# Zero rows up to 128 in the operands of the bias and mask matmuls of an attention and state-space block

## The chip, the cores and the metric

The kernel runs on one NeuronCore of a Trainium2 chip. The metric is the device time of one execution in microseconds (us), as the median of several runs; lower is better. A core has five engines that work through queues of their own, in the order in which the program lists the instructions: TensorE (PE in the profile, with its weight loads as PEld), VectorE (DVE), ScalarE (ACT), GpSimd (POOL) and SyncE (SP), which here only starts transfers. They wait for each other through semaphores.

## The reference, cut to what matters

The input `x` has 128 batches of 64 positions with 256 channels, in f32. Two blocks follow each other. The first is linear attention with a key mask, the second a selective state-space block ("Mamba"). What bears on the change is in the first block, and in the gate of the second:

```python
xn = _layernorm(x, norm_scale, norm_bias)
q, k, v = xn @ Wq + bq, xn @ Wk + bk, xn @ Wv + bv
k = where(mask, -inf, k); v = where(mask, 0.0, v)      # mask[b, t]
q = softmax(q, over the 16 channels of a head); k = softmax(k, over positions)
y = einsum(q, einsum(k, v))                            # per head and batch
h = _layernorm(y, ...) * (1 + scale) + shift           # scale, shift from cond
x = x + silu(h) @ film_out_W + film_out_b
...
shift, scale, gate = split(silu(cond) @ W_ada + b_ada, 3)
x = x + gate * mamba(permuted(_layernorm(x) * (1 + scale) + shift))
```

The state-space block has 512 channels with 16 states each. Its recurrence runs over the 64 positions of a batch.

## The kernel before, in words

The 128 batches are worked through in 16 groups of eight (512 positions, four tiles of 128). For each group `prepare` computes the attention block and the inputs of the recurrence, two calls of `scan` run the recurrence for four batches each, and two calls of `finish` project back, gate and write out. The first group is prepared in two halves of two tiles each, so its tiles are half as wide.

All of this is recorded first and issued later. `Plan.record` notes each operation as a node with what it needs; several matmuls in one `with pl.unit()` make one node. The table `ORDER` gives each node of each part a due time by hand, `Plan.order` sorts by these (a node whose buffer is not free yet steps back), and `Plan.emit` issues the nodes in that order. So the profile shows one line, L485, for nearly everything, and the groups are told apart by the names of the tiles. The engines interleave the `prepare` of one group with the `scan` and `finish` of the group before.

Names that come up below:

- `kp` (in `prepare`): the transposed keys of the group in a PSUM bank of 512 columns, one for each half of the 256 channels. A first matmul writes the mask into the bank: `lhsT=ones[0:1, :]`, `rhs=mrow`, where `mrow` is one row of 512 bf16 values, 0 or -1e30. The matmuls of `wk` and `xT`, f32 with 128 rows, then add to it. `km`, `nb`, `kT`, `ks` are the steps of the softmax that follow, on DVE, POOL and ACT.
- `project` (from line 811): `qp` (queries), `op` (the output of the attention block) and `vp` (values). For `qp` and `op` the first matmul writes the bias: `lhsT=ones` (three rows), `rhs=third[bias]`, three bf16 rows whose sum is the f32 bias, used for two tiles at a time. `vp` has no bias there.
- `gp` (in `setup`): the gate of all batches, one such bias matmul.
- `turn` makes the transposes `xtp`, `qtp`, `htp`; `ktp` transposes the keys; `ap` is keys times values, `bd` its masked copy on DVE; `yps` is queries times that.
- `hb` (in `scan`): 64-row, 64-column matmuls, 512 columns wide, that bring the inputs of the recurrence into one of two PSUM buffers; DVE's TENSOR_TENSOR_SCAN (`hs` or `hb`) runs the recurrence on them with the `decay` that ACT computes; `hs<-hs,ct` and `hs<-hs` are products and sums on POOL; `yacc` gathers the outputs on PE, started by two bf16 matmuls with the zero tile `blank`.
- `dtp`, `dt`: the step sizes; ACT writes `dt`, DMAs take it to `dt_d` in DRAM and back as `dt` in another layout, and ACT's `decay` reads that.
- `xz`, `xp`, `zp`, `pd`, `bp`, `bT`, `utp`, `w`, `diag`: other steps of the state-space block. `dm`, `ve`, `mu`, `rt`: the layer norms' small steps on POOL, from the statistics `st` of DVE.

The banks `kp`, `qp`, `op`, `vp`, `ap`, `xp` and so on share three PSUM buffers in turn (`bank`).

Every matmul is described by its rows and columns in the array: 128 rows for the f32 projections, 64 for `hb`, three for the biases, one for the mask. The constants are made at the start of `block_kernel`: `ident`, `blank`, `bmask` and others by POOL, `ones` by DVE at line 538.

Of the kernel before, what the change touches and what calls it, by code (L numbers as in the profile page):

```python
# [10 lines left out]
BF16 = mybir.dt.bfloat16  # L11
# [6 lines left out]
B, T, D, E = 128, 64, 256, 512  # L18
H, DH = 16, 16
DI, DS, DTR, DC = 512, 16, 64, 4  # L20
P = 128
NB = 8
TG = NB * T
# [465 lines left out]
def block_kernel(  # L489
# [20 lines left out]
    nc = tc.nc  # L510
# [5 lines left out]
    def ctile(shape, name, dt=F32):  # L516
        return const.tile(shape, dt, name=name, tag=name)
# [5 lines left out]
    pl = Plan(tc)  # L523
# [6 lines left out]
    def kept(shape, name, dt=F32):  # L530
        return pl.held(ctile(shape, name, dt))
# [2 lines left out]
    make_identity(nc, ident)  # L534
    blank = ctile([P, 512], "blank", BF16)
    nc.gpsimd.memset(blank, 0.0)
    ones = ctile([3, P], "ones", BF16)
    nc.vector.memset(ones, 1.0)

    bmask = ctile([P, P], "bmask")  # L540
    nc.gpsimd.memset(bmask, 1.0)
# [2 lines left out]
        out=bm3, in_=bm3, pattern=[[-DH, P // DH], [0, DH]], base=0,  # L544
# [3 lines left out]
        out=bm3, in_=bm3, pattern=[[DH, P // DH], [0, DH]], base=DH - 1,  # L548
# [20 lines left out]
    def v(name, k):  # L569
        return vec[:, VOFF[name][0] + k : VOFF[name][0] + k + 1]  # L570
# [8 lines left out]
    nA = kept([P, NC * SJ], "nA")  # L579
    gsel = kept([P, P], "gsel")  # L580
    keep = kept([P, B * T // P], "keep")
    third = {n: kept([3, D], "third_" + n, BF16) for n in ("bq", "film_out_b", "b_gate")}
    mneg_d = pl.held(dram1.tile([B, T], BF16, name="mneg_d"))
    gate_d = pl.held(dram1.tile([B, D], F32, name="gate_d"))
    mod_d = pl.held(dram1.tile([P, 4, KD, B], F32, name="mod_d"))
# [4 lines left out]
    def tile_of(shape, name, tag, bufs, dt=F32):  # L590
        return pl.tile(wp, shape, name, tag, bufs, dt)

    def bank(name):
        return pl.tile(ps, [P, 512], name, "bank", NBANK)
# [10 lines left out]
    def small(name, shape):  # L605
        return tile_of(shape, name, name, 2)
# [12 lines left out]
    def by_batch(ap):  # L619
        return ap.rearrange("p (b t) -> p b t", t=T)  # L620
# [190 lines left out]
    def project(to, srcT, w, bias, i2):  # L811

        pp = to.rearrange("p (i c) -> p i c", c=D)
        with pl.unit():
            if bias is not None:
                pl.tensor.matmul(
                    pp, lhsT=ones, rhs=third[bias][:, None, :].to_broadcast([3, 2, D]),
                    start=True, stop=False,
                )
            for h in range(2):  # L820
                i = 2 * i2 + h
                for k in range(KD):
                    pl.tensor.matmul(
                        pp[:, h, :], lhsT=srcT[:, k, i * P : (i + 1) * P], rhs=w[:, k, :],
                        start=(bias is None and k == 0),
                        stop=(k == KD - 1 and (bias is None or h == 1)),
                    )
        return pp


    def prepare(g, lo=0, NT=NT):

        NB, TG = NT * (P // T), NT * P
        tiles, cols = slice(lo, lo + NT), slice(lo * P, (lo + NT) * P)
        first = (g * TILES + lo) * (P // T)
        if lo == 0:
# [8 lines left out]
        x_d, xz, dts, uts, bT, c_d = state[g]  # L845
        xt = g4("xt", [P, NT, D])
        pl.sync.dma_start(out=xt, in_=xin[g][:, tiles, :])
        mrow = tile_of([1, TG], "mrow", "mrow", 1, BF16)
        pl.sync.dma_start(
            out=mrow, in_=mneg_d[first : first + NB, :].rearrange("(o b) t -> o (b t)", o=1)  # L850
        )
        mods = small("mods", [P, 4, KD, NB])
        pl.sync.dma_start(out=mods, in_=mod_d[:, :, :, first : first + NB])
# [11 lines left out]
        for m in range(KD):  # L865
            kp = bank("kp")[:, :TG]
            with pl.unit():
                pl.tensor.matmul(kp, lhsT=ones[0:1, :], rhs=mrow, start=True, stop=False)
                for k in range(KD):
                    pl.tensor.matmul(  # L870
                        kp, lhsT=wk[:, k, m * P : (m + 1) * P], rhs=xT[:, k, :],
                        start=False, stop=(k == KD - 1),
                    )
            km = small("km", [P, NB])
            pl.vector.tensor_reduce(km, by_batch(kp), axis=AX.X, op=ALU.max)

            nb = small("nb", [P, NB])
            pl.gpsimd.tensor_scalar(nb, km, 1.0, v("bk", m), op0=ALU.mult, op1=ALU.add)
            pl.gpsimd.tensor_scalar(nb, nb, -1.0, v("bk", m), op0=ALU.mult, op1=ALU.add)
            kk = by_batch(kT[:, m, :])  # L880
            with pl.unit():
                for b in range(NB):
                    ts = slice(b * T, (b + 1) * T)
                    pl.scalar.activation(
                        kT[:, m, ts], kp[:, ts], AF.Exp, bias=nb[:, b : b + 1]
                    )
            ks = small("ks", [P, NB])
            pl.vector.tensor_reduce(ks, kk, axis=AX.X, op=ALU.add)
            pl.vector.reciprocal(ks, ks)
            pl.gpsimd.tensor_tensor(  # L890
                kk, kk, ks[:, :, None].to_broadcast([P, NB, T]), op=ALU.mult
            )
# [3 lines left out]
        for i2 in range(NT // 2):  # L896
            pp = project(bank("vp"), xT, wv, None, i2)
            for h in range(2):
                i = 2 * i2 + h
                pl.scalar.activation(  # L900
                    vt[:, i, :], pp[:, h, :], AF.Identity,
                    scale=keep[:, g * TILES + lo + i : g * TILES + lo + i + 1],
                )
# [4 lines left out]
        for i2 in range(NT // 2):  # L908
            pp = project(bank("qp"), xT, wq, "bq", i2)
            qm = small("qm", [P, 2 * H])  # L910
            p3 = pp.rearrange("p i (h e) -> p (i h) e", e=DH)
            pl.vector.tensor_reduce(qm, p3, axis=AX.X, op=ALU.max)
            q3 = qt[:, 2 * i2 : 2 * i2 + 2, :].rearrange("p i (h e) -> p (i h) e", e=DH)
            pl.vector.tensor_tensor(
                q3, p3, qm[:, :, None].to_broadcast([P, 2 * H, DH]), op=ALU.subtract
            )
            pl.scalar.activation(q3, q3, AF.Exp)
            pl.vector.tensor_reduce(
                qs[:, i2 * 2 * H : (i2 + 1) * 2 * H], q3, axis=AX.X, op=ALU.add
            )  # L920
# [21 lines left out]
        for k in range(KD):  # L942
# [3 lines left out]
            with pl.unit():  # L946
                for i in range(NT):
                    for h in range(2):
# [3 lines left out]
                            start=True, stop=True,  # L952
# [9 lines left out]
        for i2 in range(NT // 2):  # L962
            pp = bank("yps").rearrange("p (i c) -> p i c", c=D)
            with pl.unit():
                for hi in range(2):
                    i = 2 * i2 + hi
                    for h in range(2):
                        ts = slice(h * T, (h + 1) * T)
                        for k in range(KD):
                            pl.tensor.matmul(  # L970
                                pp[ts, hi, k * P : (k + 1) * P],
                                lhsT=qT[:, k, i * P + h * T : i * P + (h + 1) * T],
                                rhs=bd[k][:, h, i, :], start=True, stop=True,
# [15 lines left out]
        for i2 in range(NT // 2):  # L989
            xs = xt[:, 2 * i2 : 2 * i2 + 2, :]  # L990
            pp = project(bank("op"), hT, wfo, "film_out_b", i2)
            pl.vector.tensor_tensor(xs, xs, pp, op=ALU.add)
# [13 lines left out]
        for m in range(KI):  # L1006
            xp = bank("xp")[:, :TG]
            with pl.unit():
                for k in range(KD):
                    pl.tensor.matmul(  # L1010
                        xp, lhsT=win[:, k, m * P : (m + 1) * P], rhs=h1[:, k, :],
                        start=(k == 0), stop=(k == KD - 1),
# [14 lines left out]
        for m in range(KI):  # L1027
            zp = bank("zp")[:, :TG]
            with pl.unit():
                for k in range(KD):  # L1030
                    pl.tensor.matmul(
                        zp, lhsT=win[:, k, DI + m * P : DI + (m + 1) * P], rhs=h1[:, k, :],
                        start=(k == 0), stop=(k == KD - 1),
# [5 lines left out]
        with pl.unit():  # L1039
            for k in range(KI):  # L1040
                pl.tensor.matmul(
                    pd[: DTR + 2 * DS, :], lhsT=wxp[:, k, :], rhs=xc[k],
                    start=(k == 0), stop=(k == KI - 1),
# [14 lines left out]
        for m in range(KI):  # L1058
            vp = bank("dtp")[:, :TG]
            pl.tensor.matmul(  # L1060
                vp, lhsT=wdt[:, m * P : (m + 1) * P], rhs=xd[:DTR, :], start=True, stop=True,
# [153 lines left out]
    for g in range(NG):  # L1215
        if g == 0:
            for lo in range(0, NT, 2):
                pl.part(prepare, f"first{lo}", g, lo, 2)
        else:
            pl.part(prepare, "second" if g == 1 else "prepare", g)  # L1220
        when = {NG - 1: "_last", 0: "_first"}.get(g, "")
        for half in range(2):
            pl.part(scan, f"scan{half}{when}", g, half)
            pl.part(finish, f"finish{half}{when}", g, half)
# [55 lines left out]
```

## Time and profile before

| what | value |
|---|---|
| median of three runs | 1940.35 us |
| lowest and highest | 1938.8 and 1941.37 us |
| the profiled execution | 1942.74 us |
| its span in the profile | 1941.0 us |
| instructions in the trace | 32381 |
| mean granted clock of TensorE | 0.987 |
| matmuls `kp<-mrow,ones` | 34, of one row |
| matmuls `qp<-third_bq,ones` and `op<-third_film_out_b,ones` | 32 each, of three rows |
| matmul `gp<-third_b_gate,ones` | 1, of three rows |

The profile comes from one execution, recorded by the hardware. Times in it are us from the start of its span. A timeline lists, for one engine, the start of an entry, its length, the engine, the line, the operation, the tiles it writes and reads, the shapes (partitions x elements; for a matmul rows*columns of the array and then the moving operand) and how many equal instructions were merged into it. A bracket at the end gives the idle time before it and who ended it. The end of a matmul is modelled, and matmuls overlap: what one costs in a stream is read from start to start, not from its length.

### The profile page before, as it was taken

To read this page: it belongs to the slowest core of one execution; us is meant where nothing else is said; L and a number is where in the kernel's file an instruction comes from. 1 tells how busy PE (TensorE), PEld (TensorE's weight loads), DVE (VectorE), ACT (ScalarE), POOL (GpSimd) and SP (SyncE) were. 2 spreads that over 40 slices of the span, in tenths; PEclk is the share of its full clock that TensorE was granted. 3 is DMA by queue.
4 is the path that set the end of the run, shared out by engine and by line. 5 is a ranking of instruction groups with operands and counts; after the bars stand their busy time and mean duration, and the time that the engine had idled before them with its cause. 6 is when DMAs were issued, how large, how long until landed. Compare 5 with 4: busy or idle time off the path is not lost. (4 is left out here: it accounts for less than half of the span.)

```text
span 1941.0 us, 32381 instructions
## 1 busy us (share of the span) xinstructions
PE 1819.4 (94%) x11304; PEld 931.0 (48%) x11304; DVE 1775.8 (91%) x1626; ACT 1696.5 (87%) x3981; POOL 1778.1 (92%) x1468
## 2 busy tenths in 40 slices
PE   7799999999999999999999999999999999999777
PEld 5453554545455454544536454454545545454233
DVE  4589799999999999999999999899999999999796
ACT  4889799898989989899898989889898998989762
POOL 3589799999999999999999999999999999999997
PEclk9899999999999999999999999999999999999998
DMA  4311322304122220312213132220412223031220
GB/s 126 97 50 45 86 72 63 86 23 125 40 86 64 68 89 26 111 55 85 64 51 93 39 99 67 77 73 22 121 39 86 67 69 87 24 115 36 81 67 22
DMA packets 173082, 135.70 MB, mean 70 GB/s; under 512 B 30804, under 2 KB 157000, under 8 KB 172920
## 3 DMA queue, kind: packets, MB, share of 16 engines
q1 hardware_dynamic: 172920, 133.64, 23.7%
q8 instruction: 90, 1.47, 0.3%
q14 instruction: 72, 0.59, 0.1%
HBM read 98.84 MB, written 34.75 MB: 69 GB/s over the span
## 5 line engine op out<-in xcount | busy, mean ns | idle before, releaser
L485 ACT ACTIVATE decay<-dt,nA 128x252 f32<-128x252 f32 x2048 | 858.4, 501 | 84.8 <-DMA dt<-dt_d 43.5
L485 POOL TENSOR_TENSOR hs<-hs,ct 128x1024 f32<-128x1024 f32 x384 | 899.5, 2363 | 19.9 <-DVE hs L485 14.8
L485 DVE TENSOR_TENSOR_SCAN hs<-decay,hb 128x1024 f32<-128x1024 f32 x384 | 863.7, 2275 | 56.9 <-PE hb L485 18.5
L485 PE MATMUL hb<-diag,uT 64*64 64x512 f32 x4096 | 531.3, 615 | 70.1 <-DVE hs L485 65.2
L485 POOL TENSOR_TENSOR hs<-hs 128x1024 f32<-128x1024 f32 x224 | 526.2, 2362 | 13.2 <-DVE hs L485 9.3
L485 DVE TENSOR_TENSOR_SCAN hb<-decay,hb 128x1024 f32<-128x1024 f32 x128 | 291.5, 2277 | 0.0
L485 PE MATMUL yacc<-hs,fold 128*64 128x256 f32 x2304 | 285.8, 391 | 4.0 <-ACT yacc L485 2.0
L485 PEld LDWEIGHTS hb<-diag,uT 64*64 64x64 f32 x4096 | 122.0, 133 | 296.1 <-DVE hs L485 129.4
L485 PEld LDWEIGHTS yacc<-hs,fold 128*64 128x64 f32 x2304 | 164.9, 139 | 122.8 <-issue 40.5
L481 ACT ACT_TABLE_LOAD x160 | 205.3, 1283 | 3.4 <-PEq L1268 0.8
L485 DVE TENSOR_TENSOR hs<-hb,ct 128x1024 f32<-128x1024 f32 x128 | 156.2, 1220 | 4.9
L485 DVE SCALAR_TENSOR_TENSOR xz<-xp,vec,xz 128x504 f32<-128x504 f32 (+5 forms) x204 | 140.9, 701 | 12.8 <-ACT xz L485 8.2
L485 POOL TENSOR_TENSOR diag<-fold,bT 128x1024 f32<-128x1024 f32 x64 | 122.0, 1907 | 10.2 <-ACT bT L485 10.2
L485 PE MATMUL zp<-h,win 128*128 128x512 f32 (+1 forms) x272 | 123.4, 580 | 1.5 <-DVE xz L485 0.6
L485 PE MATMUL xp<-h,win 128*128 128x512 f32 (+1 forms) x272 | 118.2, 578 | 2.1 <-DVE xz L485 1.1
L485 PE MATMUL yop<-wout,xz 128*128 128x256 f32 x512 | 117.7, 383 | 0.0
L485 PEld LDWEIGHTS yop<-wout,xz 128*128 128x128 f32 x512 | 94.9, 190 | 24.9 <-ACT decay L485 11.4
L485 POOL TENSOR_TENSOR w<-dt,xz 128x512 f32<-128x512 f32 (+1 forms) x68 | 81.6, 1210 | 13.0 <-ACT dt L485 12.5
L485 ACT ACTIVATE yacc<-xz,vec 128x256 f32<-128x256 f32 x128 | 60.1, 469 | 32.4 <-PE yacc L485 32.4
L485 PEld LDWEIGHTS xp<-h,win 128*128 128x128 f32 x272 | 50.7, 192 | 68.6 <-issue 50.4
L485 PEld LDWEIGHTS zp<-h,win 128*128 128x128 f32 x272 | 48.7, 190 | 62.2 <-issue 43.9
L485 ACT ACTIVATE hT<-htp,mods 128x64 f32<-128x64 f32 x256 | 77.6, 438 | 0.2
(137 smaller groups left out, 2339.4 us busy)
## 6 DMA issues: line engine op xcount, KB each, us to landing
ct<-c_d SPq DMA_DIRECT2D x128, 256.0 KB
dt<-dt_d SPq DMA_DIRECT2D x256, 128.0 KB
dt_d<-dt SPq DMA_DIRECT2D x60, 256.0 KB
ga<-gate_d SPq DMA_DIRECT2D x64, 128.0 KB
xr<-x_d SPq DMA_DIRECT2D x32, 256.0 KB
out<-xr SPq DMA_DIRECT2D x32, 256.0 KB
xt<-in_x SPq DMA_DIRECT2D x15, 512.0 KB
x_d<-xt SPq DMA_DIRECT2D x15, 512.0 KB
```

The costliest lines, as they stand in the source:

```text
L481: engine.preload_act_table_set(loaded)
L485: getattr(engine, method)(*real, **kreal)
```

## The change

The operands of the bias and mask matmuls are made 128 rows high. Rows beyond the first (mask) or the first three (bias) hold zeros, so the products are the same.

- `ones` becomes 128x128: zeros, with rows 0 to 2 set to one, by two memsets on POOL; the memset on DVE goes. The mask matmul uses all of `ones`; its rows 1 and 2 meet zero rows of the other operand.
- `mrow` is now the fixed tile `mask_rows` of 128x512, set to zero once by POOL; the DMA of each group writes its first row. It is still one buffer, taken and given back like before.
- the three tiles of `third` become 128x256, set to zero once by POOL; the DMAs write rows 0 to 2 as before.

No matmul is added, removed or moved. In the built programs the order of PE, ACT and SP is the same row by row. POOL gets six memsets among its first instructions, and its two selects on `bmask` come to stand in front of its first `dm`. DVE loses one memset, and three tiny operations on `pf` move back by one or two places. Four DMAs at the start (the first of `mrow` and of each `third`) also wait for POOL, and the first matmuls of `ones` wait for POOL in place of DVE.

```diff
-    ones = ctile([3, P], "ones", BF16)
-    nc.vector.memset(ones, 1.0)
+    ones = ctile([P, P], "ones", BF16)
+    nc.gpsimd.memset(ones, 0.0)
+    nc.gpsimd.memset(ones[0:3, :], 1.0)
+    mask_rows = ctile([P, TG], "mask_rows", BF16)
+    nc.gpsimd.memset(mask_rows, 0.0)
...
-    third = {n: kept([3, D], "third_" + n, BF16) for n in ("bq", "film_out_b", "b_gate")}
+    third = {}
+    for n in ("bq", "film_out_b", "b_gate"):
+        rows3 = ctile([P, D], "third_" + n, BF16)
+        nc.gpsimd.memset(rows3, 0.0)
+        third[n] = pl.held(rows3)
...
-                    pp, lhsT=ones, rhs=third[bias][:, None, :].to_broadcast([3, 2, D]),
+                    pp, lhsT=ones, rhs=third[bias][:, None, :].to_broadcast([P, 2, D]),
...
-        mrow = tile_of([1, TG], "mrow", "mrow", 1, BF16)
+        assert pl.slots.setdefault("mrow", 1) == 1
+        mrow = Ref(Buf([P, TG], lambda k, n=TG: mask_rows[:, :n], "mrow"))
         pl.sync.dma_start(
-            out=mrow, in_=mneg_d[first : first + NB, :].rearrange("(o b) t -> o (b t)", o=1)
+            out=mrow[0:1, :], in_=mneg_d[first : first + NB, :].rearrange("(o b) t -> o (b t)", o=1)
         )
...
-                pl.tensor.matmul(kp, lhsT=ones[0:1, :], rhs=mrow, start=True, stop=False)
+                pl.tensor.matmul(kp, lhsT=ones, rhs=mrow, start=True, stop=False)
```

## The prediction

> **What bounds the kernel now.** I began with the page's first part, the busy time of each engine. Four engines stand between 87% and 94%, so no single one carries the time, and the question is which wait ends last.
>
> ```profile
> PE 1819.4 (94%) x11304; PEld 931.0 (48%) x11304; DVE 1775.8 (91%) x1626; ACT 1696.5 (87%) x3981; POOL 1778.1 (92%) x1468
> ```
>
> From about 250 us on the kernel repeats. The same ACT instruction, `x<-xt,mu,rt`, opens at 498.92 and again at 613.05 us, a period of 114.13 us for one group of eight batches. I followed one period engine by engine in the timelines, reading only the brackets that name a wait. First ACT and POOL:
>
> ```profile
> 498.92 2.08 ACT L485 ACTIVATE x<-xt,mu,rt 128x256 f32<-128x256 f32 x4 [0.24 <-POOL mu L485]
> ...
> 550.42 0.22 ACT L485 COPY bT<-bp 128x64 f32<-128x64 f32 x1
> ...
> 559.49 2.88 ACT L485 ACTIVATE decay<-dt,nA 128x252 f32<-128x252 f32 x7 [1.17 <-DMA dt<-dt_d]
> ```
>
> ```profile
> 550.71 1.90 POOL L485 TENSOR_TENSOR diag<-fold,bT 128x1024 f32<-128x1024 f32 x1 [0.78 <-ACT bT L485]
> ...
> 562.24 2.36 POOL L485 TENSOR_TENSOR hs<-hs,ct 128x1024 f32<-128x1024 f32 x1 [0.22 <-DVE hs L485]
> ...
> 586.95 0.20 POOL L485 TENSOR_TENSOR dm<-st 128x4 f32<-128x4 f32 x1
> ```
>
> ACT shows no wait at all between 498.92 and the copy of `bT` at 550.42. POOL waits for that copy, and then works until its `mu` lets ACT start the next `x`; in those 62 us it waits 0.22 us at 562.24 and 0.13 us at 586.95 (the instruction before ends at 586.82), both times for DVE. So the period is a ring, 51.7 us of ACT and then 62.3 us of POOL, in which TensorE stands only behind those 0.35 us. TensorE itself (PE) waits in the same period for DVE or ACT: 1.71 us at 498.90, 0.41 at 529.59, 0.18 at 562.94, 0.67 at 601.77.
>
> **The change, part by part.** *What a short matmul costs.* The second period's PE timeline shows it best, because there the bursts stand beside each other:
>
> ```profile
> 122.27 0.39 PE L485 MATMUL kp<-mrow,ones 1*128 1x512 bf16 x1
> 122.59 1.99 PE L485 MATMUL kp<-xT,wk 128*128 128x512 f32 x4
> 124.50 0.39 PE L485 MATMUL kp<-mrow,ones 1*128 1x512 bf16 x1
> 124.82 1.98 PE L485 MATMUL kp<-xT,wk 128*128 128x512 f32 x4
> 126.73 0.39 PE L485 MATMUL qp<-third_bq,ones 3*128 3x512 bf16 x1
> 127.05 2.00 PE L485 MATMUL qp<-wq,xT 128*128 128x256 f32 x8
> 128.88 3.62 PE L485 MATMUL vp<-wv,xT 128*128 128x256 f32 x16
> 132.43 0.39 PE L485 MATMUL qp<-third_bq,ones 3*128 3x512 bf16 x1
> ```
>
> The sixteen `vp` follow eight matmuls of their own shape and hold PE from 128.88 to 132.43, 3.55 us; they are followed by a 3-row one. The single starts inside such a burst lie 0.215 us apart, and 16 x 0.215 = 3.44, so the change to another row count costs 0.10 us. The eight `qp` (127.05 to 128.88, 1.83 us) are followed by their own shape and pay nothing there: 8 x 0.215 = 1.72. Their extra 0.11 lies at the front: in the single rows of a like burst the starts are 442.065 (bias), 442.380, 442.700, 442.917. So a bias matmul holds PE for 0.315 us, the first full one for 0.320, and each later one for 0.215.
>
> *Price of the removed part.* With 128 rows on both sides the bias matmul has the shape of what follows it. I take 0.215 for it and 0.215 for the next. (Its 512 bf16 columns have no row without a change of shape. The bf16 pair `yacc<-blank`, 256 columns, side by side in two halves of the array, hands over after 0.23 us with its change of shape, so 0.11 to 0.13 for 256 columns.) Each removal then gives 0.100 + 0.105 = 0.205 us behind it. From below, if only the pause at the change of shape went and the next weight load stayed bare: 0.10. Above that nothing excludes a loss if the 128-row load of `ones` were bare where the 3-row one is not: a bare f32 load costs 0.105, so at worst the change gives nothing per matmul. I take 0.205, because `yps`, f32, followed by the bf16 `blank` of the same shape already shows no gap in the trace.
>
> *How many.* 34 `kp`, 32 `qp`, 32 `op` and one `gp`: 99 x 0.205 = 20.3 us. 28 of them also follow a full 128*128 matmul, and save the 0.097 of the change in front: 2.7. Together 23.0 us of PE time, 1.2% of the run. The order of the instructions on PE, ACT and SP is unchanged (the built programs agree row by row), so nothing else moves there.
>
> [...]
>
> *What reaches the end in the steady periods.* Per period four of the six lie in one stretch, `kp` at 529.59 and 537.28, `qp` at 540.53 and 556.20, worth 4 x 0.205 = 0.82. The two `op` (488.66, 490.90) lie in front of PE's 1.71 us wait for DVE at 498.90, which absorbs their 0.51: nothing. The wait at 529.59, before the first `kp`, is for ACT, which does not move. Behind the stretch PE meets these:
>
> ```profile
> 556.34 2.29 DVE L485 TENSOR_TENSOR_SCAN hs<-decay,hb 128x1024 f32<-128x1024 f32 x1 [0.30 <-PE hb L485]
> ```
>
> ```profile
> 562.94 0.44 PE L485 MATMUL qtp<-ident,qt 128*128 128x128 f32 x2 [0.18 <-ACT qt L485]
> ```
>
> At 562.94 PE waits for ACT's `qt`, which stands behind ACT's `decay` at 559.49, which waits for a DMA that ACT's own `dt` started: all of PE's lead ends there as a longer wait. What is left is DVE's lead. Its scan at 556.34 waits for `hb`. Of PE's 0.61 at that point (three matmuls) the fourth `dtp` loses about 0.3, since its bank comes free only when ACT has read the first `dtp` (ACT `dt` at 553.14, 0.66 us long); DVE gains about 0.28. That removes POOL's 0.22 at 562.24. But DVE's `bd` at 574.79 needs `ap`, which PE gives behind 562.94. How much room is there? Two periods later the same DMA came 0.86 late and PE's wait was 0.86 longer; DVE's `bd` then waited 0.44 and an earlier scan 0.23. So the room is 0.86 - 0.44 - 0.23 = 0.19 us, and no more than 0.19 reaches DVE's statistics, POOL's `dm` at 586.95 and the next ACT `x`. Twelve such periods: 12 x 0.19 = 2.3; in the four or so that are already stretched by a late DMA (115.0 to 118.0 us long) it is less, so I take 2.0 us. Bounds: nothing, and 12 x 0.35 = 4.2 (all of POOL's waits for DVE).
>
> *Before the steady part.* At 122 to 135 us PE sets the pace: DVE waits 0.95, 1.55 and 2.04 us for `kp` and `qp`. Four removals and three or four saved changes in front are worth 4 x 0.205 + 3 x 0.097 = 1.1; ACT is then busy from 135 to 166 us without a break and starts with `kt`, which also needs POOL's `kT`, so I take 0.8. At 207 to 221 DVE waits for `kp` (6.7 us) and `qp` (3.7); two to three removals on that chain, 0.7. `op` at 75.4, for which DVE waits 14.5 us, gives 0.2. Sum 1.7, bounds 0 and 3.0.
>
> *The start.* POOL gets six memsets (three of 128x256, one of 128x512, two for `ones`). They fall into its wait of 3.85 us before 6.06; with `blank` (128x512, 0.53 us) as the price of each big one and 0.20 for each small one they and the two selects of `bmask` take 4 x 0.53 + 2 x 0.20 + 0.73 = 3.3 us at the most, so they fit. If the cover were gone, it would be at most those 3.3 us, once. In the built order both selects move in front of POOL's first `dm` and out of its chain (0.34 + 0.39 us, of which some 0.6 count). `kp` and `qp` at 12 to 20 us, where the four 256-column `kp` take 2.08 us against 1.13 at 37 us, give another 0.9, but a stage that waits for weights may take either back: 0.8 us, bounds 1 us later and 2 us earlier.
>
> **Sum.** 2.0 + 1.7 + 0.8 = 4.5 us. The profiled execution took 1942.74 us (span 1941.0 and 1.7 around it), 2.4 above the median of 1940.35; so 1938.2 on its own scale and **1935.8** against the median, 0.23% less. What a measurement can tell from no change is 0.2%, 3.9 us.
>
> **The rivals.** *Swallowed* (0.27): the ring of ACT and POOL does not move, because the four banks' turns or the late DMA eat DVE's 0.28 too; only the start is left, about 1 us: 1939.5. For it: 0.19 is a small room, worked out from one odd period. *PE carries more* (0.12): banks and ACT allow the 0.82 per period through. For it: PE is the busiest engine, 94%; against it: the wait at 562.94. 12 x 0.82 = 9.8 and 2.5 before: 1928. *PE carries all* (0.03): 1940.35 - 23.0 = 1917.4. *Slower* (0.05): ACT's last `dt` (555.29, waiting 0.17 for `dtp`) comes earlier, its 256 KB write runs into the read of `dt` for which ACT waits at 559.49, and that read lands late in each period as it did in the odd one (0.87 us on the period). It decides once the read is over 0.19 us late: 12 x 0.87 = 10.4, less 2.5: 1948. That the change does not do what it says (a full-row bias matmul still pays for a change of shape) is part of Swallowed. The forecast has 0.53.
>
> **Numbers.** The forecast's own range is 1931 to 1939 by the bounds above. 1930 to 1940 leaves out the three outer cases, 0.20. Faster by over 0.2% means below 1936.5: 0.38 of the forecast's 0.53 and the two rivals below it, 0.53; slower 0.05; within 0.42.
>
> **What would show it.** Each bias matmul followed by its neighbour after about 0.215 us, and the first full matmul of the burst no longer than the rest (median and maximum of `qp` both near 380 ns, where now the maximum is 484). POOL's wait for DVE near 562 gone, PE's wait for `qt` longer by about half a microsecond, PE busy time down by up to 23 us, and the period near 113.9. If the period falls by 0.5 or more, the ring was read wrongly; if the first full matmul still takes 0.320, the price was.

## The result and the profile after

The changed kernel is slower: a median of 1946.79 us (1942.36 to 1949.68, 11 runs) against 1940.81 for the kernel before in the same comparison (1938.8 to 1942.62, 11 runs), ratio 1.0028, 95% interval 1.0018 to 1.0038. Forecast were 1935.8 us and a range of 1930 to 1940. The profiled execution after took 1944.21 us, with a span of 1942.5. From the page, the busy times, to be held against those of before:

```profile
PE 1810.7 (93%) x11304; PEld 935.2 (48%) x11304; DVE 1775.5 (91%) x1625; ACT 1697.0 (87%) x3981; POOL 1781.0 (92%) x1474
```

TensorE's work went down, as meant, by 8.7 us of busy time, and yet the end came later. First the price of a single matmul, in the second period's PE timeline (start, length, what, idle before):

```profile
117.72 0.39 PE L485 MATMUL kp<-mask_rows,ones 128*128 128x512 bf16 x1
117.94 1.88 PE L485 MATMUL kp<-xT,wk 128*128 128x512 f32 x4
119.66 0.38 PE L485 MATMUL kp<-mask_rows,ones 128*128 128x512 bf16 x1
119.87 1.88 PE L485 MATMUL kp<-xT,wk 128*128 128x512 f32 x4
121.59 0.38 PE L485 MATMUL qp<-third_bq,ones 128*128 128x512 bf16 x1
121.81 1.89 PE L485 MATMUL qp<-wq,xT 128*128 128x256 f32 x8
```

These are to be held against the prediction's lines at 122.27 to 127.05. From start to start a mask matmul now holds PE for 0.21 to 0.22 us (before 0.32), and the four matmuls behind it for 1.72 (before 1.91). That is the price that was forecast.

Next an undisturbed period, from the `x` of ACT at 610.49 to the next at 724.44: 113.95 us, where before it was 114.13. The lines that answer to those shown of before, ACT, then POOL, then DVE and PE:

```profile
610.49 2.07 ACT L485 ACTIVATE x<-xt,mu,rt 128x256 f32<-128x256 f32 x4 [0.25 <-POOL mu L485]
...
661.97 0.24 ACT L485 COPY bT<-bp 128x64 f32<-128x64 f32 x1
...
670.85 2.88 ACT L485 ACTIVATE decay<-dt,nA 128x252 f32<-128x252 f32 x7 [1.20 <-DMA dt<-dt_d]
```

```profile
662.28 1.90 POOL L485 TENSOR_TENSOR diag<-fold,bT 128x1024 f32<-128x1024 f32 x1 [0.96 <-ACT bT L485]
...
668.92 6.99 POOL L485 TENSOR_TENSOR hs<-hs,ct 128x1024 f32<-128x1024 f32 x3
...
698.31 0.20 POOL L485 TENSOR_TENSOR dm<-st 128x4 f32<-128x4 f32 x1
```

```profile
667.67 2.29 DVE L485 TENSOR_TENSOR_SCAN hs<-decay,hb 128x1024 f32<-128x1024 f32 x1 [0.39 <-PE hb L485]
```

```profile
674.30 0.44 PE L485 MATMUL qtp<-ident,qt 128*128 128x128 f32 x2 [0.40 <-DVE ks L485]
```

POOL's wait of 0.22 for DVE is gone: its three `hs` now run on without a bracket. PE's wait at `qtp` has grown (0.18 to 0.40, in the period before this one 0.65). The profile names DVE's `ks` here; the transpose reads `qt`, which ACT ended at 674.24, at about the same time. The period is 0.18 shorter, almost the 0.19 of the forecast. But few periods look like this one. The starts of `x`, in us, of five groups, in the profiled executions:

| group's `x` | before | after | after leads by |
|---|---|---|---|
| second | 166.39 | 161.51 | 4.9 |
| third | 270.19 | 266.02 | 4.2 |
| fifth | 498.92 | 495.29 | 3.6 |
| last | 1761.42 | 1761.07 | 0.35 |
| end of the span | 1941.03 | 1942.50 | -1.5 |

The lead is lost in periods like the one that starts at 495.29, which takes 115.20. The windows view shows what they have in common (a stretch, its length, busy times of PE, PEld, DVE, ACT and POOL, **PEclk**, the granted clock, and the DMA):

```profile
495.29:610.49 115.20, 111.12 (x702) 57.60 (x702) 109.70 (x98) 105.57 (x247) 110.40 (x89) 0.99 0.24 70
610.49:724.44 113.95, 109.82 (x702) 56.58 (x702) 109.71 (x98) 105.49 (x247) 110.40 (x89) 1.00 0.24 71
...
496.30:499.70 3.40, 3.40 (x15) 3.04 (x13) 2.39 (x3) 3.40 (x9) 3.40 (x2) 0.50 0.30 49
499.70:503.10 3.40, 3.40 (x30) 2.09 (x31) 2.65 (x2) 3.40 (x13) 3.40 (x3) 1.00 0.23 77
```

From 496.3 to 499.7 TensorE was granted half its clock, and full clock again behind it. The clock's records in the trace hold stretches at 0.50 that are 3.41 us or twice that (6.83) long, but for the last, which ends with the records; those of the kernel before hold one of 10.24 too. Between 250 and 1750 us, where each is 3.41 us long, the kernel before shows two, at 958.0 and 1255.0, and the changed kernel eight, at 380.2, 496.3, 725.0, 841.0, 1069.7, 1185.8, 1417.9 and 1646.6. All eight stand just behind the wait for DVE, PE's longest in most periods and 2.20 us each time, that the forecast let absorb the two `op` savings. Its line, and those behind it, in the timelines of PE and then of DVE:

```profile
495.23 1.09 PE L485 MATMUL hb<-diag,uT 64*64 64x512 f32 x8 [2.20 <-DVE hs L485]
496.25 2.07 PE L485 MATMUL rp<-yo,gsel 128*128 128x256 f32 x4
498.11 2.71 PE L485 MATMUL gtp<-gsel,x 128*128 128x128 f32 x16
```

```profile
498.36 0.69 DVE L485 TENSOR_TENSOR xr<-xr,rp 128x512 f32<-128x512 f32 x1 [1.01 <-PE rp L485]
```

The wait was 1.71 at 498.90 before and is 2.20 now. Behind it the four `rp` take 2.07 instead of 1.13, and DVE, which did not wait for `rp` in that place before, waits 1.01 us. That is most of the 1.25 us between the two periods. In the kernel before, the same lines at full clock:

```profile
499.92 1.13 PE L485 MATMUL rp<-yo,gsel 128*128 128x256 f32 x4
...
501.09 0.69 DVE L485 TENSOR_TENSOR xr<-xr,rp 128x512 f32<-128x512 f32 x1
```

### The profile page after: what moved, and what is told of

The parts are those of the page before. It is cut to its first block, busy times and chain, and to the rows that moved or that the text cites. A ratio compares the mean times of both kernels' runs of the same rounds, so it can differ in the third digit from the quotient of the medians.

```text
span 1942.5 us, 32387 instructions
## 1 busy us (share of the span) xinstructions
PE 1810.7 (93%) x11304; PEld 935.2 (48%) x11304; DVE 1775.5 (91%) x1625; ACT 1697.0 (87%) x3981; POOL 1781.0 (92%) x1474
## 5 line engine op out<-in xcount | busy, mean ns | idle before, releaser
L485 PE MATMUL hb<-diag,uT 64*64 64x512 f32 x4096 | 539.1, 623 | 73.7 <-DVE hs L485 69.1
L485 PE MATMUL yacc<-hs,fold 128*64 128x256 f32 x2304 | 280.6, 386 | 4.7 <-POOL hs L485 2.0
L485 ACT ACTIVATE h<-gtp,mods 128x64 f32<-128x64 f32 x256 | 76.8, 416 | 1.6 <-PE gtp L485 1.6
```

Of the source, the lines that this page charges most:

```text
L485: getattr(engine, method)(*real, **kreal)
```

## The experiments

**Theory A**: the two `op` matmuls that became shorter lie ahead of a wait; the wait grows from 1.71 to 2.20 us, and a stretch with that much idle time brings half clock for the next one, which delays `rp` and with it DVE and the ring. **Rival B**: matmuls over all 128 rows load TensorE more, and the clock falls by their number. **Rival C**: the memsets and larger tiles disturb the start or POOL. The runs e1 to e4 share one chip, e5 to e8 a second, e9 and e10 a third, each with runs of the kernel before beside them; these took 1944.11, 1940.28 and 1940.96 us, so kernels are compared by the ratio to them. "Drops" are stretches at half clock between 250 and 1750 us of the profiled execution.

**e1, `op` left at three rows.**

```diff
+                n = 3 if bias == "film_out_b" else P
-                    pp, lhsT=ones, rhs=third[bias][:, None, :].to_broadcast([P, 2, D]),
+                    pp, lhsT=ones[:n, :], rhs=third[bias][:n][:, None, :].to_broadcast([n, 2, D]),
```

> The changed kernel, but the output bias (op) keeps three rows; mask, query and gate biases have 128. Theory A (an idle stretch lowers the clock): the two op matmuls save 0.49 us just ahead of TensorE's wait for DVE near 495 us, the wait grows from 1.71 to 2.20 us, and a 3.41 us stretch in which TensorE idles more than about 1.7 us is followed by one at half clock. With op back at three rows the wait is about 1.7 again, so the twelve steady periods have about 2 stretches at half clock (0 to 5, since 1.7 lies on the edge) in place of 8, and the time is 1934 to 1939. Theory B (the full-row matmuls themselves bring the clock down): 67 of the 99 are still full, so 5 or 6 stretches and about 1944. Theory C (the memsets and the new tiles at the start cost it): as the changed kernel, 1946.8.

Measured: ratio 0.9998 (0.9985 to 1.0010), two drops. PE's wait is back at 1.71, though 67 of the 99 matmuls have 128 rows:

```profile
614.60 1.09 PE L485 MATMUL hb<-diag,uT 64*64 64x512 f32 x8 [1.71 <-DVE hs L485]
615.62 1.13 PE L485 MATMUL rp<-yo,gsel 128*128 128x256 f32 x4
```

The loss is gone, which speaks for A. But there is no gain either, where 1934 to 1939 us were expected: its quiet periods, but for the shorter last one, take 114.09 to 114.24. The read of `dt` for which ACT's `decay` waits came 0.3 us later than in the undisturbed period after (60.64 us behind `x` against 60.36, a wait of 1.52 against 1.20), and DVE's `bd` then waited for `ap`:

```profile
576.34 1.41 DVE L485 SCALAR_TENSOR_TENSOR bd<-ap,bv,bmask 128x512 f32<-128x512 f32 x2 [0.29 <-PE ap L485]
```

**e2, only `op` at 128 rows** (`kp` with one row, `qp` and `gp` with three).

```diff
+                n = P if bias == "film_out_b" else 3
...
-                pl.tensor.matmul(kp, lhsT=ones, rhs=mrow, start=True, stop=False)
+                pl.tensor.matmul(kp, lhsT=ones[0:1, :], rhs=mrow[0:1, :], start=True, stop=False)
```

> The changed kernel, but only the output bias (op) has 128 rows; mask, query and gate biases read one or three rows as before. Theory A: the wait is 2.2 us as in the changed kernel, 6 to 10 stretches at half clock in the twelve steady periods; the quiet periods are back at 114.1 us, and less is won before 250 us: 1946 to 1952, slower than the changed kernel or like it. Theory B: 32 of 99 are full, 3 or 4 stretches, about 1942. Theory C: 1946.8.

Measured: ratio 1.0046 (1.0029 to 1.0062), seven drops. With 32 full matmuls instead of 99 the loss is there in full, and it comes with the wait:

```profile
616.16 1.28 PE L485 MATMUL hb<-diag,uT 64*64 64x512 f32 x8 [2.20 <-DVE hs L485]
617.37 2.07 PE L485 MATMUL rp<-yo,gsel 128*128 128x256 f32 x4
```

**e3, the changed kernel with the `op` bias matmul issued three times** into the same place, the sum unchanged.

```diff
+                for left in range(3 if bias == "film_out_b" else 1, 0, -1):
+                    pl.tensor.matmul(
+                        pp, lhsT=ones, rhs=third[bias][:, None, :].to_broadcast([P, 2, D]),
+                        start=True, stop=(left > 1),
+                    )
```

> The changed kernel, and the output bias matmul is issued three times, each overwriting the one before with the same values: four more matmuls of 0.215 us in each period, just ahead of the wait, 0.86 us. Theory A: the wait falls from 2.20 to about 1.35 us, below the edge; no stretch at half clock between 250 and 1750 us except after a late transfer, quiet periods 113.95 us: 1931 to 1936, faster than the kernel before. Theory B: 64 more full-row matmuls, so more stretches at half clock: 1949 or more. Theory C: 1946.8.

Measured: ratio 0.9998 (0.9985 to 1.0011), one drop (793.7), behind a wait of ACT for `dt` that was 3.18 us long. The wait before `hb` is 1.42 from the fourth group on. So 64 more full matmuls than in the changed kernel, and fewer drops: B falls. The gain on the kernel before that was expected did not come.

**e4, the `op` bias left out**, so that the wait grows further; the output lacks `film_out_b`.

```diff
-            pp = project(bank("op"), hT, wfo, "film_out_b", i2)
+            pp = project(bank("op"), hT, wfo, None, i2)
```

> The changed kernel without the output bias at all (film_out_b is not added, so that part of the computation is left out): 0.215 us less twice in each period, again just ahead of the wait. Theory A: less work, and not faster: the wait is 2.65 us, 8 to 10 of the twelve steady periods hold a stretch at half clock, each costing 1.2 us or more: 1945 to 1951. Theory B: a third of the full-row matmuls gone, 5 or 6 stretches, about 1943. Theory C: 1946.

Measured: ratio 1.0046 (1.0031 to 1.0061), ten drops, waits of 2.49 us (2.65 expected). 32 matmuls less and no bias, and the time is 9 us longer than that of the kernel before.

**e5, the memsets and large tiles alone**; all bias and mask matmuls read three rows or one, as before (`n = 3` in e2's edit, and `ones[0:3, :]` for `gp`).

> The tiles of 128 rows and GpSimd's memsets as in the changed kernel, but every bias and mask matmul reads 3 rows or 1, as before. Theory A (TensorE's longer wait lowers the granted clock): no matmul gets cheaper, so the wait before hb stays at 1.7 us, 1 to 3 stretches at half clock lie between 250 and 1750 us, and the time is that of the kernel before less what the shorter start gives: ratio 0.998 to 1.000. Theory C (the new memsets and tiles themselves disturb the start, the places in SBUF or POOL): ratio above 1.001, as in the changed kernel.

Measured: ratio 1.0004 (0.9993 to 1.0014), two drops, wait 1.71: C does not explain the loss. The second group's `x` comes at 163.97 instead of 166.39. The early lead was then lost again behind 164.0 and 218.6 us, where this execution ran at half clock for 6.8 us each.

**e6, the kernel before with the same refill** (e3's edit, with three rows).

> The kernel before, unchanged but that its film_out_b matmul (3 rows) is issued three times over into the same place, which leaves the same sum and adds four matmuls of about 0.215 us, 0.86 us, to TensorE's work in each period of 114.13. Theory A: the wait of 1.71 before hb shrinks to about 0.85, no stretch of 3.41 us is idle by more than half any longer, so 0 or 1 stretches at half clock are left between 250 and 1750 us (2 in the kernel before); the quiet period stays 114.13; some 1 to 2 us of the first 170 us are given away, since there the added matmuls lie on the path; ratio 0.998 to 1.001. Rival (what counts is TensorE's total work, and the waits are harmless): 13 times 0.86 us, 11 us, come on top where TensorE bounds: ratio 1.003 or more.

Measured: ratio 1.0002 (0.9994 to 1.0011), no drop. The four extra matmuls per period cost nothing that can be measured (the two drops that are gone may hide a little), and the quietest periods take 114.14 and 114.15, so TensorE's total work is not the bound. The wait shrank to 1.42 and not to 0.85: from there on DVE itself waits 0.28 us for `yacc`, which stands behind `op`:

```profile
496.51 0.42 DVE L485 TENSOR_TENSOR xz<-yacc,xz 128x256 f32<-128x256 f32 x1 [0.28 <-PE yacc L485]
```

**e7, the changed kernel once more**, beside the others of the same chip.

> The changed kernel as it is, for comparison with the others of this call on one chip. Theory A: wait before hb 2.2 us, 6 to 9 stretches at half clock between 250 and 1750 us, ratio 1.000 to 1.004. If the first comparison was an accident of its chip, the ratio is below 0.999.

Measured: ratio 1.0039 (1.0026 to 1.0052), ten drops. The loss repeats.

**e8, the changed kernel with the refill only from the third group on.**

```diff
-            pp = project(bank("op"), hT, wfo, "film_out_b", i2)
+            pp = project(bank("op"), hT, wfo, "film_out_b", i2, 3 if g >= 2 else 1)
```

> The changed kernel with the film_out_b matmul (128 rows) issued three times over, but only from the third group on (g of 2 or more), where TensorE waits right behind it; the first two groups keep one. Theory A: the early lead of the changed kernel stays (x of the second group at 161 to 162 us against 166.4 before), the wait before hb is 1.3 to 1.4 us instead of 2.2, 0 or 1 stretches at half clock between 250 and 1750 us instead of 8, quiet periods 114.1 to 114.2: 3 to 7 us below the changed kernel and 1 to 5 us below the kernel before, ratio 0.9975 to 0.9995. Rival (the added 0.86 us a period lies on the path, or the drops come from the wait at 164 and 218 us that the early lead moves): ratio 1.000 or more.

Measured: 1942.15 us, 6.3 below e7 on the same chip, no drop; against the kernel before 1.0009 (0.9998 to 1.0020). So the steady loss is taken back:

```profile
496.95 1.09 PE L485 MATMUL hb<-diag,uT 64*64 64x512 f32 x8 [1.42 <-DVE hs L485]
497.97 1.13 PE L485 MATMUL rp<-yo,gsel 128*128 128x256 f32 x4
```

But no gain on the kernel before was measured; the ratio is the one that the rival was given, and one of its two reasons, the early waits, bears on it. The windows show where this execution lost its early lead, at the two waits of PE before 250 us:

```profile
161.10:164.40 3.30, 2.80 (x12) 1.19 (x13) 3.30 (x3) 3.10 (x7) 3.22 (x2) 0.50 0.17 18
164.60:167.80 3.20, 3.20 (x17) 2.70 (x20) 1.41 (x1) 2.18 (x8) 3.20 (x2) 0.50 0.00 0
215.70:219.00 3.30, 3.27 (x8) 2.61 (x8) 0.00 (x0) 3.30 (x13) 1.56 (x1) 0.50 0.60 86
```

The kernel before has the same two waits (2.38 and 2.86 us), and in its profiled execution the clock stayed full behind both. Its stretches of 3.41 us happened to divide them, at most 1.52 us of idle time in one stretch (the last section says how these lie). So single executions compare badly in this early part.

**e9, e8 and fill for these two early waits**: in one place the zeroing matmuls of `yacc` nine times over, in one place the `bq` matmul.

```diff
-            pp = project(bank("qp"), xT, wq, "bq", i2)
+            pp = project(bank("qp"), xT, wq, "bq", i2, 9 if (g, i2) == (2, 0) else 1)
...
-            yacc = onto("yacc", HB * T)
+            yacc = onto("yacc", HB * T, 9 if (g, half, m) == (0, 1, 0) else 1)
```

> The kernel with the refill from the third group on, and fill for the two early waits too: the pair of zeroing matmuls of yacc ahead of the hb at 161.60 is issued nine times over (16 added of some 0.1 us, 1.7 us), and the bq matmul ahead of the wait of 3.07 at 215.73 nine times over (8 added of 0.215, 1.7 us). Theory A: the waits of 2.68 and 3.07 shrink to 1.0 and 1.4, the two stretches at half clock at 161 (6.8 us) and 215.6 (3.4 us) go, the period from 160.93 to 268.49 is 104 to 106 instead of 107.55, and 1.5 to 4 us of time go with it: ratio to the kernel before 0.998 to 1.000, below that of the refill alone by 0.0008 to 0.002. Rival (the matmuls added there lie on the path, as the wait of DVE for them is not seen): period 107.5 or more, no gain over the refill alone.

Measured: **1935.27 us against 1940.96, ratio 0.9981 (0.9967 to 0.9995)**: below both kernels. The medians lie 5.7 us apart, the ratio stands for 3.7 us, 1.0 to 6.4. The waits are 1.80 (longer than expected) and 1.45 (timelines), and the clock stays full (windows):

```profile
158.09 1.17 PE L485 MATMUL yacc<-blank 128*64 128x256 bf16 x18
...
162.09 1.09 PE L485 MATMUL hb<-diag,uT 64*64 64x512 f32 x8 [1.80 <-DVE hs L485]
```

```profile
208.64 2.12 PE L485 MATMUL qp<-third_bq,ones 128*128 128x512 bf16 x9
...
213.93 0.38 PE L485 MATMUL qp<-third_bq,ones 128*128 128x512 bf16 x1 [1.45 <-DVE qt L485]
```

```profile
161.10:164.40 3.30, 2.31 (x19) 1.50 (x20) 3.30 (x3) 3.05 (x8) 3.14 (x4) 1.00 0.32 59
164.60:167.80 3.20, 3.19 (x30) 1.64 (x28) 3.20 (x2) 3.20 (x13) 3.20 (x2) 1.00 0.02 5
214.00:219.00 5.00, 5.00 (x29) 4.27 (x28) 2.86 (x6) 5.00 (x18) 1.56 (x2) 1.00 0.56 99
```

The period from the second `x` to the third is 103.74 instead of 107.55, and the last `x` comes at 1756.02, 5.4 us ahead of the kernel before. The profiled execution of e8 has it at 1756.22: the 3.3 us by which e9 led at the third `x` went in one period of 118.11 us with a late `dt`. So that the early fill makes the difference to e8 rests on the ratios of the runs and on the early windows. The wait of 1.80 was divided between two stretches too, with 1.43 us in one.

**e10, the refill of e8 with two instead of three**, for a wait between the 1.42 us of e8 and the 2.20 of the changed kernel.

> The kernel with the refill from the third group on, but with the film_out_b matmul issued twice instead of three times. The wait before hb is then 1.7 to 1.8 us, just at half of a stretch of 3.41. Theory A with its threshold at half a stretch (1.71): some 1 to 6 stretches at half clock between 250 and 1750 us, between the 0 of three times (wait 1.42) and the 8 and 10 of once (wait 2.20); ratio between the two kernels' 1.0009 and 1.0039. Rival (the drops are not governed by the wait's length but by something that three times happened to change): 0, or 8 to 10 as with one.

Measured: ratio 0.9999 (0.9987 to 1.0010), below the 1.0009 to 1.0039 that was expected; three drops, as expected, one of them (1018.5) behind a late `dt`. The same wait of 1.77 brings half clock behind it in one period and not in another:

```profile
494.20 1.09 PE L485 MATMUL hb<-diag,uT 64*64 64x512 f32 x8 [1.77 <-DVE hs L485]
495.22 1.13 PE L485 MATMUL rp<-yo,gsel 128*128 128x256 f32 x4
...
1184.35 1.09 PE L485 MATMUL hb<-diag,uT 64*64 64x512 f32 x8 [1.77 <-DVE hs L485]
1185.37 1.70 PE L485 MATMUL rp<-yo,gsel 128*128 128x256 f32 x4
```

The wait that ends at 494.20 is divided between two stretches. But of the six waits of 1.77 that lie whole in one, two were followed by half clock and four were not. The mark at half a stretch, 1.71 us, was an estimate of mine, and no sharp edge is shown there.

All kernels in one table (full: bias and mask matmuls over 128 rows; wait: PE's usual wait before that `hb`; clock: mean over the runs):

| kernel | full | wait, us | drops | clock | ratio to before |
|---|---|---|---|---|---|
| before | 0 | 1.71 | 2 | 0.987 to 0.988 | 1 |
| e5, memsets alone | 0 | 1.71 | 2 | 0.988 | 1.0004 |
| e6, before, refilled | 0 | 1.42 | 0 | 0.989 | 1.0002 |
| e1, `op` at three rows | 67 | 1.71 | 2 | 0.985 | 0.9998 |
| e3, refilled | 163 | 1.42 | 1 | 0.987 | 0.9998 |
| e8, refilled late | 155 | 1.42 | 0 | 0.986 | 1.0009 |
| e9, and early waits filled | 163 | 1.42 | 1 | 0.989 | 0.9981 |
| e10, refilled late, two | 127 | 1.77 | 3 | 0.985 | 0.9999 |
| after, e7 | 99 | 2.20 | 8, 10 | 0.979 | 1.0028, 1.0039 |
| e2, `op` alone | 32 | 2.20 | 7 | 0.979 | 1.0046 |
| e4, no `op` bias | 67 | 2.49 | 10 | 0.978 | 1.0046 |

Time goes with the wait and the clock, not with the number of full matmuls.

## Why the prediction was wrong

**The step that failed** is "the two `op` ... lie in front of PE's 1.71 us wait for DVE at 498.90, which absorbs their 0.51: nothing". The wait did absorb them: it grew by 0.49. But it was not free. In the profiled execution after, each of the eight stretches of 3.41 us with 2.16 to 2.20 us of idle PE between 250 and 1750 us was followed by one at half clock; in the one at 496.3 `rp` took 2.07 us instead of 1.13, 0.94 longer, and DVE waited 1.01 for it. There are eight such periods, where the kernel before has one (its other drop, 1255.0, stands behind a late `dt`), and between the third and the last group 3.8 us of lead are gone in the profiled execution. In the runs of e7's comparison, time at half clock is 80 us on average after and 47 before; it is 2 x (1 - clock) x span, as the clock's records of before and after hold only 0.50 and 1.00. Within most kernels' runs the time rises by 0.25 to 0.42 us for each us of it, so the 33 us more are 8 to 14 us: about the 11 between the forecast and the result. That last sum is a correlation; that the wait is the cause is shown by e2, e3, e4 and e8.

The other steps, in order:

- **What bounds the kernel**: the ring of ACT and POOL was read rightly. Added or removed PE work does not move the undisturbed period beyond what passes through DVE (e6: 114.14 and 114.15 with four matmuls more). That PE stands behind it only with 0.35 us was true at full clock only.
- **Price per matmul**: right (0.21 to 0.22, and 0.10 less on the first full one). "PE busy time down by up to 23" was far off on the page, 8.7, because stretches at half clock lengthen the rest; in an undisturbed period it is 110.78 to 109.82.
- **Steady periods**: 0.19 per period forecast, 0.18 measured in the quietest one, with POOL's 0.22 gone and PE's wait for `qt` longer. The others after without a drop, from the fourth group on, took 114.01, 114.39 and 114.45, and in e1 nothing came through. The sum of 2.0 us did not arrive: from the third `x` to the last e8 takes 1487.7 us and e6, the kernel before with the same refill, 1487.2, both without a drop. In e8 ACT's wait for `dt` is 1.33 to 2.65 us where the profile names that transfer, in e6 1.06 to 1.56 (leaving out a second, longer wait that the first of these periods has in both). These are single executions, but the late `dt` of the rivals Swallowed and Slower shows in them.
- **Start and early part**: mis-sized. By the second `x` 1.8 us were forecast (start 0.8, stretch at 122 us 0.8, `op` at 75.4 0.2), and 4.9 came. The start on POOL is of the forecast's size: the first full `kp` comes at 12.08 us instead of 12.89, and at 12.29 in e5, which has the memsets alone. How the rest divides is open, because the clock is in it: the profiled execution before ran at half clock from 26.2 to 29.6 us, those of after and e5 did not. So the 2.4 us by which e5's second `x` is ahead are not the memsets' alone; e1, with 67 full matmuls but such a stretch at 24.1, has it at 163.81, no earlier than e5 to speak of.
- **Rivals**: the time fell on the side of Slower, given 0.05, but by another mechanism: not a late `dt` in each period. A fall of the granted clock was not among the rivals at all, though the kernel before showed it. Its drop at 958.0 stands right behind the 1.71 us wait of that period, in which `rp` takes 1.68:

```profile
956.53 1.09 PE L485 MATMUL hb<-diag,uT 64*64 64x512 f32 x8 [1.71 <-DVE hs L485]
957.55 1.68 PE L485 MATMUL rp<-yo,gsel 128*128 128x256 f32 x4
```

That period, 115.57 us long, is one of the four that the prediction put down to a late DMA; DVE waits in it 0.61 us for `rp` and 1.14 for `hb`.
- **The range**: by the bounds as given, 1 us later at the start and nothing elsewhere, it ends at 1941.4 and not at 1939.
- **The sum**: with the early and the steady waits filled, e9 takes 1935.27 us. That it equals the forecast is luck in good part. In its profiled execution 5.0 us of lead are there at the third `x`, where 2.5 were forecast, and only 0.4 more come up to the last, where 2.0 were; and its runs have less time at half clock than those of the kernel before on its chip (42 us against 46).

What stays open: behind the last `x` the changed kernel takes 181.4 us against 179.6. e6 (182.3) and e9 (179.7) show that this part varies by as much in single executions, with 25.9 and 22.9 us at half clock in it (after 33.1, before 27.3), and no run here separates its cause.

## What to carry to other kernels

Before costing a saving at nothing because a wait of TensorE absorbs it, look at the granted clock and at how long that wait becomes: here a wait that grew from 1.71 to 2.20 us cost more than the saving (after, ratio 1.0028; e7, 1.0039; e2, 1.0046). Matmuls issued again with the same result, ahead of the wait and off the path, took the cost back (e8, 1942.15 us against 1948.42 in e7). They shortened the wait only as far as DVE did not itself have to wait for what stands behind them (1.42 us, e6). Without the change of row count a mask matmul and the four behind it held TensorE for 1.94 us instead of 2.23 (117.72 after, 122.27 before). In the steady periods next to nothing of that reached the end (from the third `x` to the last 1487.7 us in e8, 1487.2 in e6).

## What the hardware showed beyond that

Half clock came in stretches of 3.41 us, one or several together (6.83 and 10.24 us in the records of before and after). In each of these two executions all starts of half clock lie whole multiples of 3.4133 us apart, to within 0.002 us (in after 1800.174 - 69.616 is 507 x 3.4133): counted in that length, the eleven of before leave 2.27 us over, the eighteen of after 1.35. So they stand on a grid, at another phase of the program in each of the two. I laid such a grid through each of the twelve traces and took PE's idle time in each of its windows at full clock between 250 and 1750 us. Behind windows with less than 1.70 us idle no half clock followed; with 1.70 to 1.83, 6 times in 34 (in before and after alone 1 in 7); with 1.83 to 2.09, 3 in 4 (1 in 1); from 2.09 to 2.83, 37 in 37 (8 in 8). Outside that part of the program, from where the clock's records begin (19.3 us in before, 15.0 in after), the upper end holds (47 in 47 windows with more than 2.09, 9 of them in before and after), the lower does not: 26 windows with 0.90 to 1.70 us idle were followed by half clock (5 of them in before and after), among them the one at 22.7 us in the kernel before, with 1.38. What counts there beside the idle time is open. In the steady part of after, the twelve waits of 2.20 divide by how much the grid left of them in one window: with 2.16 to 2.20 us idle there half clock followed, eight times, with 1.53 to 1.79 it did not, four times. An estimate of how often, with 1.71 us as the mark, the idle time of the window ahead of the drop at 958.0 in the kernel before: (3.41 - 2.20 + 2 x 0.49) / 3.41 = 64% of the phases let at least that much of the wait fall into one window. Of the 12 such waits 8 (after) and 9 (e7) were followed by half clock.
